# A conv, Fourier-mixing and FP8 network on one core: a shorter preparation and another order for the same pieces of work

## The chip, the cores and the metric

The kernel runs on one core of one Trainium2 chip. A core has five engines, each with its own in-order instruction stream: TensorE (PE) multiplies matrices into PSUM, VectorE (DVE) and ScalarE (ACT) do elementwise work, GpSimd (POOL) does elementwise work in SBUF alone, and SyncE (SP) issues transfers. ScalarE issues transfers too, from the same stream as its computing. PSUM has eight banks. The metric is device microseconds of one execution of the whole program; lower is better. The median of three runs of the kernel before is 4435.69 us (4433.55 to 4437.77).

## The reference, cut to what matters

For each of 32 images of 56 x 56 pixels and 96 channels there are two layers. The first is an inverted residual block whose weights are mixed per image from four experts; the second mixes the pixels by a Fourier transform and ends with a small feed-forward block in FP8.

```python
rw = sigmoid(mean(x, (1, 2)) @ Wr + br)                      # 4 weights per image
h = relu(bn(x @ mix(rw, Wpw)))                               # 96 -> 384 channels
h = relu(bn(sum_i rw[i] * (depthwise3x3(h, Wdw[i]) + bdw[i])))
x = bn(h @ mix(rw, Wpwl)) + x                                # 384 -> 96
t = to_tokens(x)
h = relu(bn(layernorm(t) @ w1.T))                            # 96 -> 192
X = fft(h, axis=tokens)                                      # 3136 tokens
y = ifft(relu(X.re*rd - X.im*id + rb) + 1j*relu(X.im*rd + X.re*id + ib)).real
t = t + bn(y @ w2.T)
t = t + q(relu(q(layernorm(t) @ q(W1).T) + b1) @ q(W2).T + b2)   # q: FP8 / FP16 rounding
```

## The kernel before, in words

**Preparation** (lines 350 to 618). The weights are loaded, the batch norms folded into them, and the results kept in SBUF for the whole run. Three parts of it matter here. The table `stk16` holds the depthwise taps, spread so that each of the 128 partitions has the taps of the pixel and channels that TensorE will need there. Its source is gathered straight from the input by 16 small loads into `raw` and 4 into `rawb`, and the batch-norm vectors are gathered in the same layout by 64 loads into `v2` (`v2f` in the profile) and 16 into `v2b` (lines 433 to 454); VectorE then scales (`s2f`, `s2b`) and spreads them into `wide` and `stk16` (lines 559 to 575). The second part packs the table of the first transform: two halves are loaded into `big`, packed into `small_a` and stored to the DRAM table `dad` (lines 484 to 494). The third is the expand weights `wpw_s`, whose bias rows and the vectors `bm` are loaded element by element (lines 461 to 473). All loads are issued by SyncE. The temporary tiles live in a pool that is released before the working tiles are allocated in the same memory, so each engine's first working instruction waits for the whole preparation.

**The work of an image** (`record`, from line 686). It is cut into 566 pieces, each a few instructions of one engine: ACT's copy of the input with its sum (`pad`), the mix of the weights (`mixed`, `mix_wk2`), the expand matmuls, the depthwise convolution by TensorE in four of six channel groups (`by_tensor`: GpSimd builds `wg`, ACT's transfers `hp<-h` and `h<-hp` regroup the data, `conv` multiplies) and by VectorE in two (`by_vector`: 32 `h<-h,small,h` instructions an image, the taps), the projection (`project`), the normalization (`moments`: `turn`, `stats`, `rest`, and `root` on GpSimd), the two transforms and the spectral step (`along_h`, `along_q`, `a1` to `a4` on ACT, `d1` to `d5` on VectorE, `second`, `back_q`, `back_h`), and the feed-forward (`up`, ACT's copy, VectorE's bias, GpSimd's cast `h<-h` to FP8, `down`, and GpSimd's addition `xs<-xs,y`). The images overlap.

**The order of the pieces.** `Plan.add` records a piece with its engine, a duration in microseconds written by hand, a wanted time (`due`), and what it reads, writes and takes from the rings of buffers. `Plan.order` then plays the plan: an engine that is free starts the ready piece with the earliest wanted time whose buffers are free. `LAG` is the delay from one engine to another. `HURRY` pulls readers of PSUM forward, so that banks come free. A piece that has waited longer than `PATIENCE` for a buffer keeps later ones from taking it. The wanted times start from `WANT`, with a period of 120 us an image. What the plan yields is only the order in which the instructions are emitted; on the chip, semaphores decide when each runs. Since each is emitted through one helper, nearly all have line 310 in the profile.

Of the kernel before, what the change touches and what calls it, by code (L numbers as in the profile page):

```python
# [11 lines left out]
F32 = mybir.dt.float32  # L12
# [6 lines left out]
NE = 4  # L19
C = 96  # L20
# [128 lines left out]
class Op:  # L149
    __slots__ = ("eng", "dur", "due", "emit", "bufs", "takes", "left", "ready", "after", "end", "seq", "size", "slack")  # L150
# [3 lines left out]
LAG = {"PE": 0.12, "DVE": 0.08, "ACT": 0.1, "POOL": 0.1, "SP": 0.15}  # L154
# [13 lines left out]
WANT = dict(period=120.0, expand=0.0, vector=1.4, forward=10.7, forward_step=27.0, freq=172.2,  # L168
            freq_step=7.0, tail=259.2, tail_step=26.5, x=17.0, mix=33.5, project=33.0)

HURRY = 40.0

PATIENCE = 4.8


class Plan:
    def __init__(self):
        self.ops = []
        self.writer = {}
        self.readers = {}  # L180
# [6 lines left out]
    def add(self, eng, dur, due, emit, reads=(), writes=(), takes=(), size=0):  # L187
        op = Op()
        if eng in ("DVE", "ACT") and any(isinstance(k[0], Buf) and isinstance(k[0].ring, Banks) for k in reads):
            due -= HURRY  # L190
        op.eng, op.dur, op.due, op.emit = eng, dur, due, emit
        op.takes, op.size, op.slack = list(takes), size, 0.0
        op.after, op.ready, op.end = [], 0.0, None
        op.seq = len(self.ops)
# [23 lines left out]
    def order(self):  # L218
# [4 lines left out]
        moved = 0.0  # L223
# [11 lines left out]
        def start(op, now):  # L235
            for b in op.takes:
                b.got = b.ring.take(b.n)
            op.end = now + op.dur
            free[op.eng] = op.end
            done.append(op)  # L240
            if op.size:
                nonlocal moved
                moved = max(moved, op.end + DMA_LAG) + op.size
                push(moved, "end", op)
            else:
                push(op.end, "end", op)
# [69 lines left out]
def kernel(  # L316
# [56 lines left out]
    nc.sync.dma_start(wr_s, wr)  # L373
    wpw_s = const([C + 1, NE + 1, M], F32, "wpw_s")
    nc.sync.dma_start(wpw_s[0:C, 0:NE], wpw)
# [38 lines left out]

    dad = dram.tile([PB, NQ, 2 * KR], F32, tag="dad", name="dad")

    with tc.tile_pool(name="prep", bufs=1) as pp:
        def temp(shape, name, dt=F32):
            return pp.tile(shape, dt, tag=name, name=name)


# [10 lines left out]
        raw = temp([128, 4, 9 * NT * NE], "raw")  # L432
        v2 = temp([128, 4, 4, NT], "v2f")
        rawb = temp([128, 4, NT * NE], "rawb")
        v2b = temp([128, 4, 4, NT], "v2b")
        lo = VECS["g2"][0]
        for r in range(4):
            for s in range(4):
                at = slice(32 * r + 8 * s, 32 * r + 8 * s + 8)
                nc.sync.dma_start(  # L440
                    raw[at], stk[:, 0 : 9 * NT, :].rearrange("(g c r) k e -> r c g (k e)", g=4, r=4)[r]
                )
                for k in range(4):
                    nc.sync.dma_start(
                        v2[at, :, k],
                        vecs[:, lo + NC3 * k : lo + NC3 * k + NT].rearrange("(g c r) k -> r c g k", g=4, r=4)[r],
                    )
        for q in range(4):
            nc.sync.dma_start(rawb[q::4], stk[:, 30 : 30 + NT, :].rearrange("(g r) k e -> g r (k e)", r=4))
            for k in range(4):  # L450
                nc.sync.dma_start(
                    v2b[q::4, :, k],
                    vecs[:, lo + NC3 * k : lo + NC3 * k + NT].rearrange("(g r) k -> g r k", r=4),
                )
        rawd = temp([128, 10, NE], "rawd")
        nc.sync.dma_start(rawd[:, 0:9], stk[:, 9 * DC : 9 * DC + 9, :])
        nc.sync.dma_start(rawd[:, 9:10], stk[:, 30 + DC : 31 + DC, :])
        row_s = temp([128, NROWS], "row_s")
        nc.sync.dma_start(row_s, rows.partition_broadcast(128))
        bm = temp([C + 1, 2, M], "bm")  # L460
        for j, name in enumerate(("b1", "m1")):
            lo, hi = VECS[name]
            nc.sync.dma_start(
# [4 lines left out]
        for e in range(NE):  # L468
            nc.sync.dma_start(
# [4 lines left out]
        bp = temp([128, NE], "bp")  # L474
        nc.sync.dma_start(bp, stk[:, NSTK - 1, :])
        nc.sync.dma_start(wpwl_s, wpwl)
        nc.sync.dma_start(w1c, w1t)
        for p in range(2):
            for ri in range(2):
                nc.sync.dma_start(  # L480
                    dftb_s[2 * p + ri :: 4], dftb[S * p + NQ * ri : S * p + NQ * ri + NQ]
                )
# [4 lines left out]
        for i in range(2):  # L487
            nc.sync.dma_start(big, dfta[:, i * (NQ // 2) : (i + 1) * (NQ // 2)])
# [5 lines left out]
            nc.sync.dma_start(dad[:, i * (NQ // 2) : (i + 1) * (NQ // 2)], small_a)  # L494
        nc.vector.memset(w2b, 0.0)
        nc.sync.dma_start(w2a[0:C], w2t[:, 0, :])
        nc.sync.dma_start(w2a[C:128], w2t[0:32, 1, :])
        for j in range(2):
            nc.sync.dma_start(w2b[64 * j : 64 * j + 64, j], w2t[32:C, 1, :])
        lo = VECS["rd"][0]  # L500
        nc.sync.dma_start(fa[0:C, 0:4], vecs[0:C, lo : lo + 8 : 2], allow_slow_non_contiguous=True)
        nc.sync.dma_start(fa[C:128, 0:4], vecs[0:32, lo + 1 : lo + 8 : 2], allow_slow_non_contiguous=True)
        for j in range(2):
            nc.sync.dma_start(
                fb[64 * j : 64 * j + 64, 0:4], vecs[32:C, lo + 1 : lo + 8 : 2], allow_slow_non_contiguous=True
            )
        nc.sync.dma_start(dftc_s, dftc)
        f1 = temp([C, M], "f1")
        nc.sync.dma_start(f1, fw1t)
        f2 = temp([128, NC3, C], "f2")  # L510
        nc.sync.dma_start(f2, fw2t)
# [20 lines left out]
        s2f = temp([128, 4, NT], "s2f")  # L532
        bn_scale(s2f, v2[:, :, 0], v2[:, :, 3], EPS_CONV)
        s2b = temp([128, 4, NT], "s2b")
        bn_scale(s2b, v2b[:, :, 0], v2b[:, :, 3], EPS_CONV)
        s2d = temp([128, 1], "s2d")
        bn_scale(s2d, vec("g2")[:, DC : DC + 1], vec("v2")[:, DC : DC + 1], EPS_CONV)
# [19 lines left out]

        nc.gpsimd.memset(stk16, 0.0)
        wide = temp([128, 4, NT, 4, 4, NE], "wide")
        nc.gpsimd.memset(wide, 0.0)  # L560
        for s in range(4):
            pw, ph = divmod(s, 2)
            for i in range(3):
                v = wide[:, :, :, 1 - pw + i, 1 - ph : 4 - ph, :].rearrange("p g c j e -> p (g c) (j e)")
                t = raw.rearrange("p g (c i j) -> p (g c) i j", i=3, j=3 * NE)[:, :, i, :]
                nc.vector.scalar_tensor_tensor(v, t, of_pixel[:, s : s + 1], v, ALU.mult, ALU.add)
        tap16 = stk16[:, :, 0 : 16 * NG].rearrange("p e (c g t) -> p e g c t", g=4, t=16)
        for t in range(16):
            bw, bh, qw, qh = t >> 3, t >> 2 & 1, t >> 1 & 1, t & 1
            for e in range(NE):  # L570
                nc.any.tensor_mul(tap16[:, e, :, :, t], wide[:, :, :, 2 * bw + qw, 2 * bh + qh, e], s2f)
        bias = stk16[:, :, 16 * NG : 17 * NG].rearrange("p e (c r) -> p e r c", r=4)
        for e in range(NE):
            nc.vector.tensor_mul(bias[:, e], rawb.rearrange("p r (c e) -> p r c e", e=NE)[:, :, :, e], s2b)
        bn_shift(bias[:, NE], v2b[:, :, 1], v2b[:, :, 2], s2b, "sh2")
        nc.vector.tensor_scalar_mul(stk16[:, 0:NE, 17 * NG], bp, s3)
        bn_shift(stk16[:, NE, 17 * NG : 17 * NG + 1], vec("b3"), vec("m3"), s3, "sh3")

        for e in range(NE):
            nc.vector.tensor_scalar_mul(stk16[:, e, NSM : NSM + 10], rawd[:, :, e], s2d)  # L580
        bn_shift(
            stk16[:, NE, NSM + 9 : NSM + 10], vec("b2")[:, DC : DC + 1], vec("m2")[:, DC : DC + 1], s2d, "sh2d"
# [27 lines left out]

        nc.vector.tensor_copy(fw1, f1, saturate=False)
# [74 lines left out]
    def record(b):  # L686
# [42 lines left out]
        def spread():  # L729
# [7 lines left out]
            "PE", 0.12, t0 - WANT["mix"] - 2,  # L737
# [17 lines left out]
        def mix_wk2():  # L755
# [8 lines left out]
            "DVE", 2.6, t0 - WANT["mix"], lambda: mixed(wk.ap, wpw_s, wpw_s[:, NE], C + 1),  # L764
# [3 lines left out]
            "DVE", 1.5, t0 - WANT["mix"], lambda: mixed(small.ap, stk16, stk16[:, NE], 128),  # L768
# [3 lines left out]
        add("DVE", 3.0, t0 + 5, mix_wk2, reads=[(mix, 2)], writes=[(wkc, 0)], takes=[wkc])  # L772
# [15 lines left out]
        def by_vector(h, c, due, acc):  # L788
# [42 lines left out]
            for i in range(2):  # L831
                parts = [(hv, k) for k in ((0, 1), (1, 2, 3))[i]]
                if i == 0:
# [3 lines left out]
                    "ACT", cols("ACT", T), at - 3, lambda i=i: first(i), reads=[*parts, (small, 0)],  # L837
                    writes=[(acc, i)], takes=[acc] if i == 0 else [],
                )
                for k, tap in enumerate((0, 1, 2, 3, 5, 6, 7, 8)):  # L840
                    add(
                        "DVE", 1.06, at + 2 * k, lambda i=i, tap=tap: one(i, tap), reads=[*parts, (small, 0)],
# [4 lines left out]
        def by_tensor(h, c, due, hid):  # L847
# [47 lines left out]
            def conv():  # L895
# [13 lines left out]
                "PE", 4.0, due, conv, reads=[(wg, 0), *((hp, r) for r in range(4))],  # L909
# [23 lines left out]
        for h in range(2):  # L933
# [36 lines left out]
            for c in range(NC3):  # L970
                add(
                    "PE", 3.0, due - (200 if c else 0), lambda c=c, f=project: f(c),
# [19 lines left out]
        def moments(p, of, key, due, out_extra):  # L992
# [27 lines left out]
            add("PE", 0.75, due, turn, reads=[key], writes=[(ps, 0)], takes=[ps, ln])  # L1020
            add("DVE", 1.26, due + 1, stats, reads=[(ps, 0)], writes=[(ln, 0)])
            add("DVE", 0.7, due + 1, rest, writes=[(ln, 0)])
            add("POOL", 2.1, due + 1, root, writes=[(ln, 0)])
# [3 lines left out]
        for st in range(NS):  # L1027
# [6 lines left out]
                "POOL", 1.2, due + 10,  # L1034
# [18 lines left out]
            for q0, nq in ((0, 4), (4, 3)):  # L1053
# [11 lines left out]
                def scaled(q0=q0, nq=nq, ps=ps, ha=ha, ln=ln):  # L1065
# [8 lines left out]
                    "PE", 0.31 * nq, due, hidden, reads=[(xh[h], k), (ln, 0)], writes=[(ps, 0)], takes=[ps, ha],  # L1074
                )
                add(
                    "DVE", 0.33 * nq, due + 1, scaled, reads=[(ps, 0), (ln, 0)], writes=[(ha, 0)],
# [3 lines left out]
                def along_h(q0=q0, nq=nq, ps=ps, ha=ha, da=da):  # L1081
# [11 lines left out]
                    "PE", 0.88, due + 3, along_h, reads=[(ha, 0), (da, 0), (da, 1)], writes=[(ps, 0)], takes=[ps, g],  # L1093
# [24 lines left out]
        for i, (k0, nk) in enumerate(GROUPS):  # L1118
# [12 lines left out]
            for blk, f, rz, n in ((0, fa, r_za, nk), (1, fb, r_zb, nb)):  # L1131
# [62 lines left out]
                ca, cd = cols("ACT", n * S), cols("DVE", n * S)  # L1194
# [5 lines left out]
                add("DVE", cd, due + 2 + blk, d1, reads=[(z, 0)], writes=[(tmp, 0)])  # L1200
                add("ACT", ca, due + 2 + blk, a4, writes=[(tmp, 1)])
                add("DVE", cd, due + 2 + blk, d4, reads=[(tmp, 0)], writes=[(z, 0)])
                add("DVE", cd, due + 3 + blk, d5, reads=[(tmp, 1)], writes=[(z, 1)])
# [299 lines left out]
```

## Time and profile before

| | |
|---|---|
| median of three runs | 4435.69 us |
| the profiled execution | 4425.4 us |
| its span, first to last instruction | 4423.4 us |
| TensorE busy | 4026.5 us (91%) |
| VectorE busy | 3599.7 us (81%) |
| ScalarE busy | 2517.5 us (57%) |
| GpSimd busy | 1763.6 us (40%) |
| mean granted TensorE clock | 0.954 |

A busy share is a mean over the whole span. The page also shows it in 40 slices of some 111 us as tenths, where 9 is 90% or more; the row PEclk shows the granted TensorE clock in the same slices. A row of waits names the waiting engine and what it writes, after the arrow the engine whose work ended the wait, and then the sum in microseconds, how often, and the longest. A row of a group gives the engine, the operation, its output and inputs, the shape, how often it ran, then busy time and the mean of one in ns, then the idle time before it. Names ending in "q" (SPq, ACTq) stand for the issuing of transfers.

### The profile page before, as it was taken

Reading aid. Unit: us, or ns where it says so; the run is one execution under the profiler, and the core shown is the slowest. Engines: PE = TensorE matmul, PEld = TensorE weight load, DVE = VectorE, ACT = ScalarE, POOL = GpSimd, SP = SyncE. Lnnn points to the kernel's source line nnn. Section 1 sums busy time; section 2 is a strip of 40 time slices with the busy share of each in tenths; the row PEclk is TensorE's granted clock in tenths of the full one; section 3 lists DMA queues with packets and bytes.
Section 4 is the critical chain, followed back from the end, with each engine's and each line's share of the span. In section 5 each row is a group of like instructions: output and inputs, shape, how many; then the busy total and the mean of one; then the engine's idle time right before and its main releaser. Section 6 shows DMA issues by size and latency. Waiting matters only on the chain.

```text
span 4423.4 us, 114239 instructions
## 1 busy us (share of the span) xinstructions
PE 4026.5 (91%) x44802; PEld 2551.4 (58%) x44802; DVE 3599.7 (81%) x9731; ACT 2517.5 (57%) x4971; POOL 1763.6 (40%) x1360
## 2 busy tenths in 40 slices
PE   1898999999999999999999999999999999999985
PEld 0465555665555665655565666566565566565563
DVE  5677788887788888888888888888888888878865
ACT  1365555566555666555656655565665555655553
POOL 1123444343444343444434444444444443444423
PEclk9898999999999999999999999999999999999997
DMA  3775877776877767787776787777678777677652
GB/s 79 135 168 142 182 175 165 166 163 159 180 176 160 172 168 166 181 178 164 172 170 158 177 183 182 162 173 163 163 176 180 165 163 163 162 170 173 157 140 73
DMA packets 441668, 719.40 MB, mean 163 GB/s; under 512 B 166090, under 2 KB 299530, under 8 KB 441130
## 3 DMA queue, kind: packets, MB, share of 16 engines
q1 hardware_dynamic: 391978, 495.24, 43.3%
q10 hardware_dynamic: 49152, 216.86, 27.1%
q8 instruction: 353, 5.78, 0.6%
q14 instruction: 185, 1.52, 0.1%
HBM read 286.08 MB, written 209.01 MB: 112 GB/s over the span
## 4 chain that ended last, share of the span: by engine, by line
PE 54%; DVE 14%; DMA 10%; ACT 9%; POOL 6%; issue 3%; SPq 2%; ACTq 1%; POOLq 0%; DVEq 0%
PE ps L310 54%; DVE h L310 4%; POOL h L310 3%; DVE ln L310 3%; DMA hp<-h 3%; DVE nt L310 3%; DMA out_dram<-xs 3%; POOL ln L310 2%; ACT tmpa L310 2%; DMA dd<-in_dftd_dram 2%; ACT h L310 1%; DMA xs<-xd 1%; ACT za L310 1%; ACTq L310 1%; ACT tmpb L310 1%
## 5 line engine op out<-in xcount | busy, mean ns | idle before, releaser
L310 DVE SCALAR_TENSOR_TENSOR h<-h,small,h 128x784 f32<-128x784 f32 x1024 | 1106.9, 1114 | 32.3 <-ACT h L310 24.4
L310 POOL CAST h<-h 128x784 fp8e5<-128x784 f16 x384 | 534.2, 1395 | 800.6 <-DVE h L310 790.2
L310 PE MATMUL ps<-x,wk 97*32 97x435 f32 (+2 forms) x4608 | 735.6, 601 | 17.0 <-DVE tmpb L310 13.1
L310 PE MATMUL ps<-hp,wg 32*32 32x392 f32 x16384 | 522.0, 515 | 38.6 <-issue 33.7
L310 POOL TENSOR_TENSOR xs<-xs,y 96x784 f32<-96x784 f32 x128 | 422.4, 3300 | 299.0 <-DVE y L310 277.1
L310 ACT ACTIVATE h<-ps 128x435 f32<-128x435 f32 (+2 forms) x768 | 400.4, 531 | 242.6 <-PE ps L310 225.0
L310 ACT ACTIVATE hp<-ps,small 128x392 f32<-128x392 f32 x512 | 267.2, 587 | 363.1 <-PE ps L310 274.8
L310 PE MATMUL ps<-dftb_s,g 112*64 112x112 f32 (+1 forms) x3776 | 416.3, 280 | 29.2 <-ACT tmpb L310 25.1
L310 POOL TENSOR_TENSOR ln<-ln,mhalf 120x7 f32<-120x7 f32 (+1 forms) x256 | 427.6, 1670 | 21.3
L310 DVE SCALAR_TENSOR_TENSOR ha<-ps,ln,nshift 120x192 f32<-120x192 f32 x896 | 306.4, 407 | 157.6 <-PE ps L310 153.1
L310 PEld LDWEIGHTS ps<-dftb_s,g 112*64 112x64 f32 (+1 forms) x3776 | 346.3, 167 | 142.4 <-issue 66.5
L310 POOL TENSOR_SCALAR ln<-ln 120x7 f32<-120x7 f32 (+1 forms) x256 | 89.3, 349 | 813.6 <-DVE ln L310 805.0
L310 PEld LDWEIGHTS ps<-hp,wg 32*32 32x32 f32 x16384 | 294.9, 105 | 202.0 <-issue 95.2
L310 PE MATMUL ps<-h,wk 32*96 32x392 f32 x4096 | 382.8, 519 | 0.7 <-DMA h<-hp 0.6
L310 DVE BATCH_NORM_STATS2 ln<-ps 120x6 f32<-120x96 f32 (+1 forms) x1792 | 318.0, 247 | 63.4 <-PE ps L310 63.2
L310 PEld LDWEIGHTS <-fw 96*128 96x128 fp8e5 (+1 forms) x1536 | 148.1, 113 | 369.7 <-issue 307.5
L310 ACT ACTIVATE h<-h 128x784 f32<-128x784 f32 x128 | 109.8, 858 | 439.4 <-DVE h L310 409.6
L310 PEld LDWEIGHTS ps<-x,wk 97*32 97x32 f32 (+1 forms) x4608 | 196.0, 122 | 277.5 <-issue 178.2
L310 ACT CAST h<-ps 128x784 f16<-128x784 f32 x384 | 305.3, 815 | 85.7 <-POOL h L310 65.5
L310 PE MATMUL ps<-w1c,x 96*120 96x192 f32 x1792 | 348.9, 342 | 2.7 <-DVE tmpb L310 1.0
L310 PEld LDWEIGHTS ps<-w1c,x 96*120 96x120 f32 x1792 | 302.4, 190 | 63.3 <-issue 30.7
L310 DVE TENSOR_SCALAR nt<-ps,ln 112x96 fp8e5<-112x96 f32 x896 | 266.8, 368 | 53.5 <-POOL ln L310 53.5
(178 smaller groups left out, 7275.4 us busy)
## 6 DMA issues: line engine op xcount, KB each, us to landing
hp<-h ACTq DMA_DIRECT2D x512, 217.5 KB
h<-hp ACTq DMA_DIRECT2D x512, 196.0 KB
gd<-g SPq DMA_DIRECT2D x384, 192.0 KB
g<-gd SPq DMA_DIRECT2D x192, 336.0 KB
dd<-in_dftd_dram SPq DMA_DIRECT2D x128, 343.0 KB
xd<-park SPq DMA_DIRECT2D x128, 294.0 KB
xs<-xd SPq DMA_DIRECT2D x128, 294.0 KB
yt<-yd SPq DMA_DIRECT2D x128, 294.0 KB
```

Of the source, the lines that this page charges most:

```text
L310: return self.tc.keep_in_program_order(method(*args, **kwargs))
```

## The change

The preparation takes the taps in one load, `rawp`, in the layout of the input; VectorE scales them there with the batch norm into `plain`, with the shift as a fifth column; `plain` goes to DRAM, and the 20 gathering loads read it back. The scaling after the spreading becomes a copy. The packing of `big` is written last, and most loads are issued by ScalarE.

In the plan, `port` marks VectorE's pieces with two SBUF inputs and all of GpSimd's, and only one of them runs at a time in the plan. Durations, lags, `HURRY`, `PATIENCE` and the period change, and a table `NUDGE` of 566 numbers is added to the wanted times, the same for each image. Which instructions an image consists of does not change.

```diff
-LAG = {"PE": 0.12, "DVE": 0.08, "ACT": 0.1, "POOL": 0.1, "SP": 0.15}
+LAG = {"PE": 0.1, "DVE": 0.06, "ACT": 0.06, "POOL": 0.08, "SP": 0.12}
-WANT = dict(period=120.0, ...
+WANT = dict(period=120.1, ...
-HURRY = 40.0
-PATIENCE = 4.8
+HURRY = 66.6
+PATIENCE = 1.6
+NUDGE = [
+    38, -0.7, 37.2, -3.6, -60, 38.9, -9, -64.3, 52.5, -3, 2.8, 5.8, 25, 15.7, -3.8, 2.9, -15.8, -29.5,
...
+]
     def add(self, eng, dur, due, emit, reads=(), writes=(), takes=(), size=0, port=False):
         op = Op()
+        op.seq = len(self.ops)
+        due += NUDGE[op.seq % len(NUDGE)]
...
+        op.port = port or eng == "POOL"
...
-            op.end = now + op.dur
+            if op.port:
+                nonlocal port
+                op.end = port = max(port, now) + op.dur
+            else:
+                op.end = now + op.dur
```

```diff
-        for r in range(4):
-            for s in range(4):
-                at = slice(32 * r + 8 * s, 32 * r + 8 * s + 8)
-                nc.sync.dma_start(
-                    raw[at], stk[:, 0 : 9 * NT, :].rearrange("(g c r) k e -> r c g (k e)", g=4, r=4)[r]
-                )
-                for k in range(4):
-                    nc.sync.dma_start(
-                        v2[at, :, k],
-                        vecs[:, lo + NC3 * k : lo + NC3 * k + NT].rearrange("(g c r) k -> r c g k", g=4, r=4)[r],
-                    )
...
+        rawp = temp([128, NSTK, NE], "rawp")
+        nc.sync.dma_start(rawp, stk)
         bm = temp([C + 1, 2, M], "bm")
...
-            nc.sync.dma_start(
+            nc.scalar.dma_start(
                 bm[C : C + 1, j].rearrange("o (c p) -> o c p", p=128),
...
-        nc.sync.dma_start(wpwl_s, wpwl)
-        nc.sync.dma_start(w1c, w1t)
+        nc.scalar.dma_start(wpwl_s, wpwl)
+        nc.scalar.dma_start(w1c, w1t)
...
-        for i in range(2):
-            nc.sync.dma_start(big, dfta[:, i * (NQ // 2) : (i + 1) * (NQ // 2)])
+        def pack(i):
+            nc.scalar.dma_start(big, dfta[:, i * (NQ // 2) : (i + 1) * (NQ // 2)])
...
+        for c in range(NT):
+            nc.vector.tensor_scalar_mul(plain[:, 9 * c : 9 * c + 9, 0:NE], rawp[:, 9 * c : 9 * c + 9], s2[:, c : c + 1])
+            nc.vector.tensor_scalar_mul(plain[:, 9 * NT + c, 0:NE], rawp[:, 10 * NC3 + c], s2[:, c : c + 1])
+        nc.vector.tensor_copy(plain[:, 9 * NT :, NE], sh2[:, 0:NT])
...
+        nc.sync.dma_start(plain_d, plain)
+        raw = temp([128, 4, 9 * NT, NE + 1], "raw")
+        rawb = temp([128, 4, NT, NE + 1], "rawb")
+        for r in range(4):
+            for s in range(4):
+                nc.sync.dma_start(
+                    raw[32 * r + 8 * s : 32 * r + 8 * s + 8].rearrange("c g k e -> c g (k e)"),
+                    plain_d[:, 0 : 9 * NT].rearrange("(g c r) k e -> r c g (k e)", g=4, r=4)[r],
+                )
+        for q in range(4):
+            nc.sync.dma_start(
+                rawb[q::4].rearrange("g r k e -> g r (k e)"),
+                plain_d[:, 9 * NT :].rearrange("(g r) k e -> g r (k e)", r=4),
+            )
...
+        for i in range(2):
+            pack(i)
```

```diff
-            "DVE", 2.6, t0 - WANT["mix"], lambda: mixed(wk.ap, wpw_s, wpw_s[:, NE], C + 1),
+            "DVE", 2.57, t0 - WANT["mix"], lambda: mixed(wk.ap, wpw_s, wpw_s[:, NE], C + 1), port=True,
-        add("DVE", 3.0, t0 + 5, mix_wk2, ...
+        add("DVE", 2.0, t0 + 5, mix_wk2, port=True, ...
-                        "DVE", 1.06, at + 2 * k, lambda i=i, tap=tap: one(i, tap), ...
+                        "DVE", 1.02, at + 2 * k, lambda i=i, tap=tap: one(i, tap), port=True, ...
-                "PE", 4.0, due, conv, ...
+                "PE", 3.75, due, conv, ...
-            add("POOL", 2.1, due + 1, root, writes=[(ln, 0)])
+            add("POOL", 1.8, due + 1, root, writes=[(ln, 0)])
-                "POOL", 1.2, due + 10,
+                "POOL", 0.84, due + 10,
-                ca, cd = cols("ACT", n * S), cols("DVE", n * S)
+                ca, cd = cols("ACT", n * S) + 0.06, cols("DVE", n * S) - 0.06
...
-                    "POOL", 1.1, due + 9.5,
+                    "POOL", 0.84, due + 9.5,
-                "POOL", 2.0, due + 15,
+                "POOL", 1.67, due + 15,
```

In the last part the three GpSimd durations are those of the copy to `park`, of the cast to FP8 and of the addition to `xs`; `d1`, `d4` and `d5` get `port=True`. The other durations on TensorE, of `turn`, `hidden`, `along_h`, `second`, `back_q`, `back_h`, `turn_back`, `up`, `down` and `project`, fall or rise by up to 20% in the same way.

## The prediction

> **What bounds the kernel now.** I read the page first, then a table by stretch of the span, then the waits of TensorE in the steady part, then the chain through the preparation, last GpSimd's operations by shape.
>
> The page, busy time and slices:
>
> ```profile
> span 4423.4 us, 114239 instructions
> PE 4026.5 (91%) x44802; PEld 2551.4 (58%) x44802; DVE 3599.7 (81%) x9731; ACT 2517.5 (57%) x4971; POOL 1763.6 (40%) x1360
> PE   1898999999999999999999999999999999999985
> PEclk9898999999999999999999999999999999999997
> ```
>
> TensorE is the bound everywhere but in the first slice (preparation) and the last two (drain). The table by stretch (columns: stretch, its length, busy PE, PEld, DVE, ACT, POOL, then granted clock, DMA share, GB/s):
>
> ```profile
> 0.00:60.00 60.00, 0.00 (x0) 0.00 (x0) 25.78 (x136) 3.21 (x10) 9.38 (x18) 1.00 0.25 51
> 60.00:100.00 40.00, 2.29 (x5) 1.40 (x6) 22.48 (x103) 4.97 (x10) 0.00 (x0) 1.00 0.46 122
> 1000.00:2000.00 1000.00, 946.42 (x10583) 596.31 (x10582) 842.50 (x2255) 601.24 (x1190) 418.45 (x318) 0.96 0.75 171
> 2000.00:3000.00 1000.00, 951.46 (x10674) 598.38 (x10673) 856.15 (x2261) 598.89 (x1171) 433.52 (x324) 0.97 0.74 171
> 3000.00:4000.00 1000.00, 939.36 (x10545) 599.82 (x10547) 838.32 (x2262) 600.42 (x1195) 413.81 (x314) 0.96 0.73 167
> ```
>
> So there are two things to win. One is the preparation: almost no TensorE work before 99 us. The other is 54.3 us of TensorE idle in each 1000 (mean of the three rows), and with it the clock. The granted clock is 0.963 there; if all busy time scaled with it, the missing 0.037 of 945.7 us is 35 us per 1000. The period of an image comes from the chain: its piece "13.40 PE ps x178" stands at 529.93 and again at 4079.37, 27 images later, so 131.5 us. Without idle and at full clock it would be 131.5 x (1 - 0.054 - 0.035) = 119.8 us. That is the floor, 11.7 us an image below now. What ends TensorE's idle time from 1000 to 4000 us:
>
> ```profile
> PE ps L310 <- POOL h L310: 41.7, 40, 1.7
> PE ps L310 <- DVE ln L310: 26.1, 24, 1.9
> PE ps L310 <- issue: 25.8, 17, 3.3
> PE ps L310 <- ACT tmpb L310: 17.7, 23, 1.4
> PE ps L310 <- ACT tmpa L310: 15.6, 22, 0.7
> ```
>
> None is long, and the counts (23 images lie in it) say that the same places stall in image after image: errors of a fixed order, not one missing resource. The largest is the last cast on GpSimd before the `down` matmuls. That cast and the residual addition, in the steady part (first two) and in the drain, where VectorE is mostly idle (last two):
>
> ```profile
> L310 POOL CAST h<-h 128x784 fp8e5<-128x784 f16 x276 | 399.6, 1452 | 580.7 <-DVE h L310 576.3 <-DMA da<-dad 4.3
> L310 POOL TENSOR_TENSOR xs<-xs,y 96x784 f32<-96x784 f32 x91 | 311.1, 3419 | 201.3 <-DVE y L310 191.9 <-DMA yt<-yd 9.4
> L310 POOL CAST h<-h 128x784 fp8e5<-128x784 f16 x18 | 15.9, 888 | 27.3 <-DVE h L310 27.3
> L310 POOL TENSOR_TENSOR xs<-xs,y 96x784 f32<-96x784 f32 x6 | 10.0, 1664 | 13.1 <-DVE y L310 13.1
> ```
>
> Beside VectorE they take 1452 and 3419 ns, alone 888 and 1664. The plan of before counts 1.1 and 2.0 us, so it is short by 0.35 and 1.4 us where it matters.
>
> The chain of the preparation:
>
> ```profile
> 66.47 5.07 DMA big<-in_dfta_dram
> 76.96 5.91 DMA big<-in_dfta_dram
> 87.93 2.86 DMA dad<-small_a
> 99.23 1.11 PE ps L310
> ```
>
> Until 66.5 us the chain is SyncE issuing small transfers one after another; then two loads of `big`, two packings on VectorE (4.9 us each), two stores; at 91.05 the first instruction of the plan may start, and it waits for all of the preparation.
>
> **What the Trainium skill says.** GPSIMD Engine Reference, "8. Key points": it shares its SBUF interfaces with VectorE and contends with instructions of two SBUF inputs. The four rows above agree (1452 against 888 ns). TensorE: Matmul & The Clock Gate, "HAM oscillation — how this bites in real kernels": idle gaps let the array's clock fall. The trace agrees in sign: 0.963 in the steady part, 0.67 from 4350 to 4400 us, where gaps of 2 to 4 us lie. DMA: Bandwidth & Descriptors, "Two DMAs through the same engine are not ordered": a transfer that reads another's output has to wait for its completion; `raw<-plain_d` will do so.
>
> **The change, part by part.** First the preparation. Removed are 80 small loads of `v2f` and `v2b`, 20 of `raw` and `rawb` from the input, `rawd` and `bp`: SyncE's 3.98 to 49.2 us and 60.3 to 62.2 us. Added are one load `rawp`, a scaling on VectorE into `plain`, its store, 20 loads from it. 25 loads move to ACT's queue. I walk the new order with durations of the rows of before.
> - ACT's queue: `bm` and the bias rows of `wpw_s` 10.6 us (49.71 to 60.32 before), `wpwl_s` to `dftb_s` 4.2, `w2a` to `f` 6.8, some 2.5 of waits for earlier transfers: done at 24. Then one table load (1.28) and the square roots (1.9): 27.4; `big` is issued behind them at 28 and lands at 33.
> - VectorE in its order waits for `fa`, `fb`, `f1`, `f2`, so it reaches the reciprocals at 26.9. Reciprocals and products 8 us, five 0.56 us products for `wpw_s`, some ten operations of 0.15 to 0.2: `plain` is ready at 39.4.
> - Store and landing 1.8 (as `wd<-wkc`: 104.11 to 105.93): 41.2. Loads of `raw` at 0.33 each. Meanwhile VectorE scales `wpwl_s` and the rest (5.3) and packs the first half of `big` (4.9): 49.6.
> - The second load of `big` waits for that packing and takes 5.4: 55. Here is a wait that the diff doesn't show: each transfer waits for the one eight places before it in issue order, and the fifteenth load of `raw` follows `big` on the same semaphore. So two loads of `raw` and all four of `rawb` (0.6 each) sit behind it on SyncE until 58.2, and the first store of `dad`, in the same queue, until 61.4.
> - `wide` then runs 57.8 to 61 and the copies to 61.7. The second packing needs the first store landed and ends at 66.6; the second store takes 3.2: 69.8.
> The plan would start at 70 instead of 91: 21 us less. Bounds: without that coupling 64 (27 less); with slower loads on ACT's queue and one more landing of 2 to 3 us at each of three dependent steps 78 (13 less). Nothing covers or hides this stretch, so it goes to the end in full.
>
> Second, the plan. No instruction of the 32 images changes in kind or size: 566 pieces an image in both. What changes is their order, through four inputs. Exclusion with the durations of a free port: VectorE's port pieces are 32 x 1.02 + 2.57 + 2.0 + 12.7 (three of the nine pieces of a spectral step, by `cols` less 0.06) = 50 us an image, GpSimd's 8 x 1.8 + 12 x 0.84 + 4 x 1.67 + 4 x 0.84 + 4.4 + 0.5 = 39. Together 89 of a period of 120, so the rule fits. GpSimd was busy 422 us in 1000, 55 us an image: 16 us of stretching that the old plan knew only as flat averages. TensorE's pieces get durations near the rows (`conv` 3.75; its 128 records span 3.6 to 3.7 at full clock). The lags fall by 0.02 to 0.04 us, `HURRY` rises and `PATIENCE` falls, and a table moves each piece's wanted time by 16 us on average. I can't read a time out of an order. Bounds from the trace: nothing (the new order stalls as often), and all of 11.7 us an image. I take half. The stalls recur in the same places, which is what an order with truer durations removes; but of the idle listed above only the GpSimd row and part of the ACT and VectorE rows stand where the plan's numbers were wrong, DMA is busy 0.74 of the time with its model unchanged, and VectorE at 84% leaves little room to catch up. Half is 5.9 us x 31 periods = 183 us. Fill and drain (99 to 240 us and 4211 to the end) I leave, at 10 us either way: chains of single pieces there.
>
> Sum, against the profiled execution: span 4423.4 - 21 - 183 = 4219. Its own time was 4425.4, and the median of the runs shown is 10.3 above that; carried over, 4435.7 - 204 = 4232.
>
> **Rivals.**
> - *Preparation alone.* The order is different and not better. For: the places that wait by ACT and VectorE are short chains that any dense order meets again. Against: the GpSimd waits. 4435.7 - 21 = 4415, from 4395 to 4423.
> - *Nearly the floor.* The search found an order that the chip follows; 0.85 of 363 us: 4435.7 - 21 - 309 = 4106. For: recurrent stalls, and a clock that rises as gaps close. Against: DMA and VectorE as above.
> - *Slower.* VectorE falls behind a plan that counts its taps at 1.02 us, where the row shows 1114 ns: 32 x 0.094 = 3 us an image. If these do not overlap idle time, the projections, which wait for the taps, stand 3 us each image: 31 x 3 - 21 = 72 us more, 4508. It decides from 0.7 us an image on (21 / 31). Against: exclusion already books GpSimd's time on the same port, and VectorE has 16% idle to give.
> - *The preparation does not shrink*, as `plain_d` adds a dependent trip: only with the upper bounds twice over; not separate.
>
> **How the numbers follow.** Half, meaning a gain of 2.5 to 8.5 us an image: 0.60, 4152 to 4340. Nearly the floor 0.16. Preparation alone or little more (to 2.5 us) 0.16. Slower 0.08. The range 4115 to 4400 leaves out about 0.08 below and 0.12 above. A run tells 0.2%, 9 us, from no change: faster 0.90, same 0.02, slower 0.08.
>
> **What would show it.** First plan instruction near 70 us, with `raw`'s last loads behind the second `big`; the period 125 to 126 us; TensorE idle near 27 us in 1000 with a clock of 0.98; the wait for POOL `h` gone from the head of the list; POOL's cast nearer 1.1 us. Wrong: a period of 131, or of 121; new waits of TensorE by DMA.

## The result and the profile after

| | before | after |
|---|---|---|
| median of the runs, us | 4434.62 | 4577.98 |
| profiled execution, its own time / its span, us | 4425.4 / 4423.4 | 4554.42 / 4552.7 |
| first instruction of the plan, us | 91.05 | 72.98 |
| period of an image, us | 131.5 | 137.45 |
| TensorE idle in 1000 us of the steady part | 54.3 | 76.8 |

The changed kernel is slower: ratio 1.0324, 95% interval 1.0275 to 1.0373. The forecast was 4232 us.

The period is read in every kernel from the one `pooled` piece on VectorE that each image has: in after it starts at 1020.2 and, 22 images later, at 4044.2 us. 31 periods that are 6.0 us longer make 185 us more, and the preparation 18 less. Fill and drain are shorter: span less start less 31 periods is 219 us in after and 256 in before. Together 185 - 18 - 37 = 130, as the two spans have it (129.3); the medians differ by 143.

The page of after, its busy times and slices:

```profile
span 4552.7 us, 114486 instructions
PE 4085.5 (90%) x44802; PEld 2665.0 (59%) x44802; DVE 3500.7 (77%) x9663; ACT 2521.9 (55%) x4982; POOL 1710.1 (38%) x1361
PE   2999999999998999999999999999999999999985
PEclk9999999999998999999999999998999999999986
```

TensorE got its first work earlier (a 2 in the first slice), and its busy time rose by 59 us with the same 44802 matmuls. The table by stretch (stretch, length, busy PE, PEld, DVE, ACT, POOL, granted clock, DMA share, GB/s) says that the clock fell too:

```profile
0.00:60.00 60.00, 0.95 (x2) 0.40 (x2) 30.30 (x115) 2.68 (x8) 9.60 (x19) 1.00 0.39 96
1000.00:2000.00 1000.00, 918.39 (x10064) 598.90 (x10067) 776.08 (x2126) 567.29 (x1123) 387.41 (x302) 0.93 0.69 160
2000.00:3000.00 1000.00, 924.96 (x10220) 607.49 (x10198) 791.80 (x2211) 580.15 (x1150) 395.40 (x309) 0.94 0.70 162
3000.00:4000.00 1000.00, 926.40 (x10320) 605.73 (x10310) 787.83 (x2152) 565.80 (x1112) 402.04 (x308) 0.94 0.71 164
```

All engines do less in 1000 us, and TensorE is still the busiest of them. What ends TensorE's idle time from 1000 to 4000 us (total, times, longest):

```profile
PE ps L356 <- DVE tmpa L356: 66.0, 43, 2.5
PE ps L356 <- ACT g L356: 57.2, 21, 4.5
PE ps L356 <- DVE ha L356: 40.8, 65, 1.1
PE ps L356 <- ACT h L356: 21.7, 24, 1.2
```

The wait for GpSimd's `h`, 41.7 us before, is gone, and its cast is short; both were forecast (the cast and the residual addition by shape: count, then busy us and mean ns):

```profile
L356 POOL TENSOR_TENSOR xs<-xs,y 96x784 f32<-96x784 f32 x88 | 387.2, 4400 | 256.3 <-DVE y L356 256.3
L356 POOL CAST h<-h 128x784 fp8e5<-128x784 f16 x261 | 273.4, 1051 | 921.3 <-DVE h L356 901.9 <-DVE mix L356 19.4
```

In their place stand other waits, again about as many as there are images or a small multiple: a new order with stalls of its own at fixed places. The addition takes 4400 ns, longer than the 3419 of before, where the plan, with the exclusion of the port, counts 1670.

The preparation did what was forecast. SyncE's issues in after:

```profile
44.49 0.35 SPq L592 DMA_DIRECT2D plain_d<-plain  x1
46.06 12.95 SPq L597 DMA_DIRECT2D raw<-plain_d  x16
59.05 2.56 SPq L602 DMA_DIRECT2D rawb<-plain_d  x4
61.71 8.53 SPq L514 DMA_DIRECT2D dad<-small_a  x2
72.98 1.60 SPq L356 DMA_DIRECT2D da<-dad  x4
```

The sixteen loads of `raw` take 12.95 us, held behind the second `big` as the walk had it, and the plan's first instruction comes at 72.98, 3 us after the forecast.

One more view differs more than any other. ScalarE's waits that a transfer ended, from 1000 to 4000 us; in before the largest are

```profile
ACT hp L310 <- DMA h<-hp: 38.2, 6, 7.1
ACT h L310 <- DMA hp<-h: 16.2, 4, 5.5
```

and 82 us in all; in after

```profile
ACT h L356 <- DMA yt<-yd: 79.5, 11, 7.5
ACT h L356 <- DMA g<-gd: 72.5, 18, 4.7
ACT g L356 <- DMA h<-hp: 49.8, 10, 5.9
ACT h L356 <- DMA hp<-h: 44.8, 11, 8.5
```

and 295 us in all. One such place, in ScalarE's order of time (start, duration, what, idle time before):

```profile
2191.96 7.72 ACTq L356 DMA_DIRECT2D hp<-h  x5
2199.73 1.61 ACT L356 ACTIVATE h<-h 128x784 f32<-128x784 f32 x2 [7.24 <-DMA yt<-yd]
```

`hp<-h` doesn't read `yt`. In the compiled program the transfers of SyncE and ScalarE take eight semaphores in turn, and one that gets a semaphore waits for its last user, eight places earlier in the common order of issue. The trace shows it here: the last of the five `hp<-h` has the semaphore of a `yt<-yd` that landed at 2199.16, and is issued at 2199.18. The Trainium skill, DMA: Bandwidth & Descriptors, "Why a DMA increments its semaphore by 16 and not by 1", gives a reason for such a wait: with two transfers in flight on one semaphore, a count doesn't tell which has landed. The traces show the wait; no run here leaves it out. ScalarE stands still meanwhile, and its evictions stand behind it.

### The profile page after: what moved, and what is told of

The parts are those of the page before. It is cut to its first block, busy times and chain, and to the rows that moved or that the text cites. A ratio compares the mean times of both kernels' runs of the same rounds, so it can differ in the third digit from the quotient of the medians.

```text
span 4552.7 us, 114486 instructions
## 1 busy us (share of the span) xinstructions
PE 4085.5 (90%) x44802; PEld 2665.0 (59%) x44802; DVE 3500.7 (77%) x9663; ACT 2521.9 (55%) x4982; POOL 1710.1 (38%) x1361
## 4 chain that ended last, share of the span: by engine, by line
PE 63%; DVE 13%; DMA 8%; ACT 6%; issue 4%; POOL 3%; ACTq 2%; SPq 1%; POOLq 0%; DVEq 0%
PE ps L356 63%; DMA yt<-yd 5%; DVE ha L356 3%; DVE nt L356 3%; POOL xs L356 2%; DVE h L356 2%; ACT h L356 2%; ACTq L356 1%; ACT tmpa L356 1%; DVE za L356 1%; DMA out_dram<-xs 1%; DVE tmpa L356 1%; DMA hp<-h 1%; ACT tmpb L356 1%; DVE zb L356 1%
## 5 line engine op out<-in xcount | busy, mean ns | idle before, releaser
L356 POOL CAST h<-h 128x784 fp8e5<-128x784 f16 x384 | 395.7, 1034 | 1304.2 <-DVE h L356 1278.5
L356 PE MATMUL ps<-x,wk 97*32 97x435 f32 (+2 forms) x4608 | 686.4, 570 | 3.2 <-DVE wk L356 3.2
L356 POOL TENSOR_TENSOR xs<-xs,y 96x784 f32<-96x784 f32 x128 | 531.2, 4150 | 376.7 <-DVE y L356 373.5
L356 PE MATMUL ps<-hp,wg 32*32 32x392 f32 x16384 | 562.2, 558 | 23.6 <-issue 13.2
L356 PEld LDWEIGHTS ps<-hp,wg 32*32 32x32 f32 x16384 | 324.0, 109 | 204.4 <-issue 124.4
L356 PE MATMUL ps<-dftb_s,g 112*64 112x112 f32 (+1 forms) x3776 | 440.0, 291 | 1.5 <-ACT hp L356 1.1
L356 PEld LDWEIGHTS ps<-dftb_s,g 112*64 112x64 f32 (+1 forms) x3776 | 369.5, 176 | 109.0 <-issue 47.9
L356 POOL TENSOR_TENSOR ln<-ln,mhalf 120x7 f32<-120x7 f32 (+1 forms) x256 | 396.3, 1548 | 21.3
L356 ACT ACTIVATE tmpa<-ps,fa 128x224 f32<-128x224 f32 (+1 forms) x448 | 210.7, 499 | 206.7 <-PE ps L356 199.2
L356 PE MATMUL ps<-dd,yt 116*96 116x112 f32 x1792 | 241.3, 297 | 80.2 <-ACT g L356 71.7
```

What stands on the lines that cost most here:

```text
L356: return self.tc.keep_in_program_order(method(*args, **kwargs))
```

## The experiments

The planner is arithmetic over its durations, so each kernel also has a planned period: from where the plan ends images 3 and 28. "Gap" is the measured period less the planned one. Half clock is the time from 1000 to 4000 us in which the trace's clock record grants TensorE 0.5. `e_plan`, `e_actsp_tap` and the two runs with an added stall are given below. A run's profiled execution need not be its median, so small differences of period and of median do not match exactly.

| kernel | median us | planned period | period | gap | TensorE idle in 1000 | half clock, us |
|---|---|---|---|---|---|---|
| before | 4434.6 | 127.9 | 131.5 | 3.6 | 54.3 | 215 |
| after | 4578.0 | 128.6 | 137.45 | 8.8 | 76.8 | 396 |
| e_prep | 4409.3 | 127.9 | 131.2 | 3.3 | 53.7 | 208 |
| e_prep_actsp | 4337.1 | 127.9 | 129.8 | 2.0 | 49.6 | 212 |
| e_actsp | 4461.7 | 128.6 | 134.0 | 5.4 | 61.4 | 379 |
| e_dur | 4583.0 | 128.4 | 137.05 | 8.6 | 76.2 | 263 |
| e_durport | 4689.4 | 135.8 | 140.7 | 4.9 | 86.2 | 393 |
| e_nonudge | 4687.0 | 134.7 | 140.8 | 6.1 | 88.4 | 372 |
| e_jit_a | 4429.9 | 130.0 | 133.1 | 3.1 | 58.9 | 184 |
| e_jit_b | 4629.3 | 133.3 | 139.7 | 6.4 | 89.8 | 369 |
| e_pe | 4646.6 | 133.6 | 139.5 | 6.0 | 86.4 | 348 |
| e_peold | 4517.4 | 131.9 | 135.0 | 3.0 | 75.5 | 215 |

**The two parts apart.** `e_prep` is before with the hunks of the diff inside and just ahead of the `prep` pool; `e_plan` is before with all the others.

> The new preparation with the plan of before, instruction for instruction. My step for the preparation, corrected by the trace of after (first instruction of the plan at 73 instead of 91 us): 4434.6 - 18 = 4417 us, period of an image unchanged at 131.5 us. If the new preparation had a cost later on (where its constants lie, what its transfers leave behind for the first images), the time would be 4430 or more.

> The new plan with the preparation of before. If the two parts add up, 4578 + 18 = 4596 us, with the period of 137.5 us that the trace of after shows. If the plan was harmed by what the new preparation left behind, it would come out at 4450 or less.

Measured: `e_prep` 4409.3 us, ratio to before 0.9942 (0.9922 to 0.9962); `e_plan` 4584.6 us, 1.0349 (1.0315 to 1.0383), period 137.8. The preparation gains 17 to 35 us and does no harm later; the whole loss is the plan's. The question is what in the plan loses 4578.0 - 4409.3 = 169 us against `e_prep`.

**ScalarE behind its own transfers.** The order of all engines stays; only the issuing queue changes:

```diff
-                    lambda r=r: se.dma_start(
+                    lambda r=r: sy.dma_start(
                         hp.ap[32 * r : 32 * r + 32].rearrange("p g n -> p (g n)"), hg.ap[r::4, :]
...
-                    lambda q=q: se.dma_start(
+                    lambda q=q: sy.dma_start(
                         hid.ap[32 * q : 32 * q + 32].rearrange("p r n -> p (r n)"),
```

> The changed kernel with the same order on every engine, but the transfers between h and hp that ScalarE issues are issued by SyncE, at their place in the plan's order. Theory A (ScalarE stands in its queue behind its own transfers, each waiting for an earlier one: 295 us of such waits from 1000 to 4000 in after, 82 in before, and its evictions then come late to TensorE): the period falls from 137.5 to about 131, 4578 - 6 x 31 = about 4390 us, unless SyncE now holds other transfers back. Theory B (the waits of ScalarE are cover, the order itself stalls TensorE): 4530 to 4620 us, with TensorE's waits for tmpa, g and ha as in after.

> The control of e_actsp: the plan of before and the new preparation (e_prep, 4409 us), with the transfers between h and hp issued by SyncE. Theory A (ScalarE standing behind its own transfers is what the new order made worse): the old order has few such waits (98 us from 1000 to 4000 in e_prep, 295 in after), so the gain is small, 10 to 40 us: 4370 to 4400. Theory S (any order gains by taking these transfers off ScalarE, and e_actsp says nothing on the change): about the 116 us that after gained, near 4295 us.

Measured: `e_actsp` 4461.7 us, 116 less than after; `e_prep_actsp` 4337.1 us, 72 less than `e_prep` and 0.9774 (0.9740 to 0.9808) of before: the fastest kernel of this study. Both lie between their two theories. ScalarE's waits for transfers fall to 65 and 8 us. What ended TensorE's idle time in `e_actsp`:

```profile
PE ps L356 <- DVE tmpa L356: 69.8, 46, 2.5
PE ps L356 <- DVE ha L356: 51.0, 67, 1.1
PE ps L356 <- issue: 27.2, 17, 3.6
PE ps L356 <- ACT h L356: 23.0, 25, 1.0
PE ps L356 <- DVE nt L356: 14.6, 44, 0.5
```

The wait for `g`, 57 us, is gone; those for `tmpa`, `ha` and `nt` are as in after. Without the control, theory A would seem nearly right. With it, most of the gain turns out to be open to the old order too: of the 169 us only 116 - 72 = 44 come from the new order meeting these waits more often. The other 4461.7 - 4337.1 = 125 us are in the order itself. The edit takes two things off ScalarE at once, the waits and the issuing (392 us of its queue from 1000 to 4000 in after, 428 in `e_prep`); no run parts them.

In the plan one can see what `tmpa` is. TensorE's `up` wants two neighbouring PSUM banks; a forward transform has just taken one of them, and `up` stands until VectorE has evicted it. The stall is in the plan's own arithmetic, 2.44 us once in each image, and on the chip; TensorE's order of time in `e_actsp`:

```profile
997.45 0.92 PE L356 MATMUL ps<-dftb_s,g 112*128 112x112 f32 x6
1000.88 1.46 PE L356 MATMUL ps<-n,fw 96*128 96x392 fp8e5 x4 [2.51 <-DVE tmpa L356]
```

It is not a surprise to the plan, but an order that it made.

**The steps of the plan, one after the other.** `e_dur` is `e_prep` with the new durations, lags and period only; `e_durport` adds the exclusion; `e_nonudge` adds the new `HURRY` and `PATIENCE`; the table makes it after.

> The new preparation with only the new durations and lags in the plan: no exclusion, no table, HURRY and PATIENCE as before. This is the step of my prediction on its own: an order made with truer durations. Theory M (mine: truer durations remove recurring stalls): a period below 131.2 us and a time below the 4409 us of e_prep, about 4320 if it is half of what I took. Theory P (what the plan's own clock does not know, transfers and clock, stays, and shorter TensorE pieces take away its reserve): planned period 128.4 plus a gap of 3.6 to 6 us, so 132 to 134.4 us, 4430 to 4510 us.

> e_dur with the exclusion of the shared port added to the plan, still without the table and with HURRY and PATIENCE as before. The plan's own clock gives a period of 135.8 us instead of 128.4. Theory X (the exclusion books time that the chip does not lose, and the order follows the plan): 135.8 + 3.6 to 6 us a period, 4650 to 4730 us. Theory Y (the exclusion is true, and what it books the chip loses anyway): the gap to the plan closes, 136 to 137 us, at the level of e_dur if e_dur has 136 too, else 4560 us.

> The changed kernel without its table: NUDGE is not added to the wanted times; exclusion, durations, lags, HURRY and PATIENCE stay. The plan's own clock gives 4423 us for it, against 4219 with the table and 4229 for before; the chip needed 3.6 us an image more than the plan for before and 8.9 more for after. Theory T (the table fits the plan's arithmetic and not the chip): without it the chip follows the plan as closely as it did before, 134.7 + 3.6 = 138.3 us an image, about 4600 us. Theory D (the gap of 8.9 us comes with the exclusion and the durations): 134.7 + 8.9 = 143.6 us an image, about 4760 us.

```diff
 e_durport against after
-        due += NUDGE[op.seq % len(NUDGE)]
-HURRY = 66.6
-PATIENCE = 1.6
+HURRY = 40.0
+PATIENCE = 4.8
 e_dur against e_durport
-        op.port = port or eng == "POOL"
+        op.port = False
```

Measured, step by step: durations and lags +174 us (4583.0), exclusion +106 (4689.4), `HURRY` and `PATIENCE` -2 (4687.0, no difference), table -109 (4578.0). So the durations, which my forecast counted on, cost more than the whole loss, and more than either theory had: M was below 4409, P ended at 4510. The exclusion comes on top, and theory X holds for it: it books time. It doesn't keep the pieces apart on the chip either: GpSimd's addition takes 2535 ns with it and 2458 without. `e_nonudge` falls between theories T (4600) and D (4760). The table is no mere misfit: it wins 109 us, though the plan's own clock promised 204. Each step makes a new order, so these figures belong to this sequence of steps; the next runs show how much an order alone can do.

**Why truer durations lose.** Two runs change nothing but the wanted times, by at most 0.3 us; two split the durations.

```diff
 e_jit_a, e_jit_b against e_prep (566 random numbers from -0.3 to 0.3 in JIT)
+        due += JIT[len(self.ops) % 566]
 e_pe against e_prep (twelve such edits)
-                "PE", 4.0, due, conv, reads=[(wg, 0), *((hp, r) for r in range(4))],
+                "PE", 3.75, due, conv, reads=[(wg, 0), *((hp, r) for r in range(4))],
 e_peold against e_dur: the same twelve, back
```

> e_prep (4409 us, 131.2 us an image) with each piece's wanted time moved by a random amount of at most 0.3 us, the same for all images; durations, lags, HURRY and PATIENCE of before. The plan's own clock gives 130.0 us an image instead of 127.9. Theory Q (the order of before is a picked one: the smallest change of the wanted times reorders everything and costs time, whatever the durations say): 130.0 plus a gap of 3.6 to 8.9 us, 133.6 to 138.9 us, 4485 to 4650 us. Theory N (0.3 us of wanted time are nothing to the chip; what e_dur lost came from its durations): 4385 to 4435 us.

> As e_jit_a with other random amounts, also at most 0.3 us; the plan's own clock gives 133.3 us an image. Theory Q: 136.9 to 142.2 us an image, 4585 to 4750 us. Theory N: 4385 to 4435 us.

> e_prep with only the new durations of TensorE's pieces in the plan (122.9 us of TensorE planned in an image before, 117.7 now); no other new duration, lag, exclusion or table. The plan's own clock gives 133.6 us an image. Theory P (the longer pieces are a reserve that keeps the chip near its plan; without it the gap widens to that of e_dur, 8.6 us): 142.2 us an image, about 4750 us. Theory Q (the gap has nothing to do with TensorE's durations): 3.6 to 6 us of gap, 137 to 139.5 us, 4590 to 4670 us.

> e_dur with the durations of TensorE's pieces as before: new are those of VectorE, ScalarE and GpSimd and the lags. The plan's own clock gives 131.9 us an image. Theory P: the gap goes back to 3.6 us, 135.5 us an image, about 4545 us, below e_dur's 4583 although its plan is longer by 3.5 us an image. Theory Q: a gap of 5 to 9 us like that of other orders, 137 to 141 us, 4590 to 4710 us.

Measured: `e_jit_a` 4429.9, `e_jit_b` 4629.3, `e_pe` 4646.6, `e_peold` 4517.4 us. `e_jit_a` came out where theory N had it and below theory Q. But `e_jit_b` is 220 us slower than `e_prep` though no wanted time moved by more than 0.3 us and no duration changed. Its waits of TensorE begin with one stall of 4.5 us in every image:

```profile
PE ps L314 <- DVE tmpa L314: 103.4, 23, 5.0
PE ps L314 <- DVE ln L314: 50.2, 45, 1.3
PE ps L314 <- ACT g L314: 48.5, 19, 4.2
```

So theory N falls. The planner is greedy, and each image's pattern is repeated 32 times: a minute change at one decision gives another pattern, here 20 and 220 us worse. Both random tables give planned periods above the 127.9 of before, 130.0 and 133.3 us. That fits an order of before that was picked among many, a pick that new durations lose; with two tables it is not shown. The durations don't add up either: those of TensorE alone cost 237 us (`e_pe`), the others alone 108 (`e_peold`), both together 174.

Theory P holds in part. `e_peold` came out where P had it. The gap is 2.0 to 3.6 us for five of the six kernels planned with the old durations of TensorE and 4.9 to 8.8 for the six planned with the new ones. But `e_jit_b`, with the old ones, has 6.4, and `e_pe`, for which P expected 8.6, has 6.0. Much of the gap is in TensorE's busy time; this is accounting, not an experiment. The pieces add up to 122.9 us an image with the old durations and to 117.7 with the new ones. On the chip (idle column and period) an image takes 0.923 x 137.45 = 126.9 us of TensorE in after, 124.4 in before. If TensorE is busy all through the half clock, it loses half of that time: 396 / 2 / 3000 x 137.45 = 9.1 us an image in after, an estimate, which leaves 117.8. So the new durations are true, at full clock; the chip runs 132 of 1000 us at half clock, and the plan doesn't know it. The old ones were too long by somewhat less than what the clock takes in before (3.2 against 4.7 us).

Idle time completes the account. In after the plan has TensorE idle for 128.6 - 117.7 = 10.9 us an image and the chip for 10.6, so there the whole gap is busy time. `e_durport` plans 18.1 us of idle and has 12.1: where a plan has more idle time, part of the longer busy time fits into it. And in `e_dur` the clock explains only 6.0 of 8.9 us of longer busy time; the rest stays open.

**VectorE.** One of the eight taps that VectorE does for a piece is not issued, in the order of `e_actsp`; the output lacks that term.

```diff
-                        "DVE", 1.02, at + 2 * k, lambda i=i, tap=tap: one(i, tap), port=True, reads=[*parts, (small, 0)],
+                        "DVE", 1.02, at + 2 * k, lambda i=i, tap=tap: one(i, tap) if tap != 3 else None, port=True, reads=[*parts, (small, 0)],
```

> e_actsp (4462 us, period 134.0 us) with one of the eight VectorE taps of each piece not issued, so that part of the depthwise sum is left out: 4 x 1.1 = 4.4 us of VectorE less in each image, in the same order. My rival Slower (VectorE falls behind a plan that counts its taps at 1.02 us): the rest of the loss goes, the period falls to about 131 us and the time to about 4370. Theory B (the order itself waits for PSUM banks and for short chains at fixed places, and the clock falls after these): 4430 to 4465 us, TensorE's waits for tmpa, ha and nt as in e_actsp.

Measured: 4454.1 us, period 133.7, against 4461.7 and 134.0. The taps that stay grow from 1120 to 1174 ns, so VectorE's busy time falls by 2.4 us an image (3494.2 to 3418.8 us), not by 4.4, and that brings 0.3: my rival's mechanism is not at work in this order. GpSimd's addition falls from 3486 to 1851 ns in the same run, so its length isn't what the order waits for either.

**One added stall.** The base is `e_prep_actsp`. Ahead of the first conv of an image ScalarE copies a small tile onto itself eight times, and TensorE runs one matmul of four columns, into the bank that conv then overwrites; in `e_hold` that matmul reads the copied tile, in `e_free` another.

```diff
+            for _ in range(8):
+                se.copy(pad, pad)
+            te.matmul(ps.bank()[:C, 0:NE], pad[0:96], pad[0:96, 0:NE], start=True, stop=True)
```

> e_prep_actsp (4337 us, 129.8 us an image) with eight small copies added on ScalarE ahead of the first conv of each image (about 2 us of ScalarE) and one tiny matmul on TensorE that waits for none of them. The control of e_hold: what the copies alone cost. ScalarE is idle 40% there, so 0 to 1 us an image: 4337 to 4370 us.

> e_free, but the tiny matmul reads what the eight copies write, so TensorE stands still once in each image, at the first conv, for some 2 us. Theory K (a stall costs more than its own length, because stretches of half clock follow it): against e_free, 2 us of stall and 2 to 5 us of clock an image, 31 x 4 to 7 = 124 to 217 us more, and more half-clock stretches between 1000 and 4000 us (27 in e_prep_actsp, 61 in after). Theory L (a stall costs at most its own length; TensorE catches up later): 0 to 2 us an image, 0 to 62 us more, and as many half-clock stretches.

Measured: 4344.9 us, as expected, and 4466.0, 121 us apart, or 3.9 us for each of 31 periods (3.1 by the periods of the two traces). The stall was longer than meant; the waits of TensorE in `e_hold`:

```profile
PE ps L310 <- ACT pad L310: 93.3, 22, 4.4
PE ps L310 <- POOL h L310: 46.2, 46, 1.8
PE ps L310 <- issue: 5.2, 5, 1.8
```

It is 4.24 us each time, and in exchange 22 us of waits put down to issue go (27.5 in `e_free`), so 3.2 us an image are net. The number lies just under theory K's 124 to 217 us, and that for a stall twice as long as K reckoned with: a stall costs about its own net length, nothing of it is caught up, and the clock adds little. Half-clock stretches do become more, 42 instead of 29, but half clock only goes from 222 to 263 us, and (263 - 222) / 2 / 3000 x 133 = 0.9 us an image. The Trainium skill (TensorE: Matmul & The Clock Gate, "HAM oscillation — how this bites in real kernels") warns of idle gaps above about 3.4 us; one of 4.2 us in 133 us shows the sign, not the doubling of after.

The traces say more on the doubling. In all sixteen of them the clock record changes only on a fixed grid of 3.41 us. I sort the grid's windows between 1000 and 4000 us that begin at full clock by whether TensorE is busy for less than 0.6 of the window:

| kernel | windows under 0.6 | of these, half clock follows | other windows | of these, half clock follows |
|---|---|---|---|---|
| before | 26 | 24 | 789 | 6 |
| after | 52 | 47 | 709 | 14 |
| e_free | 30 | 26 | 783 | 2 |
| e_hold | 47 | 39 | 754 | 3 |

So what goes with half clock is a thinly used window. A single gap of 3.4 us is not needed: before has none above 3.3 us there, and its clock still falls 30 times. After has twice as many such windows as before, and 1.8 times the half clock.

## Why the prediction was wrong

**Preparation: right.** 18 us of the 21, within its bounds; `e_prep` confirms it alone. ScalarE's queue took until 31 instead of 24 us and `plain_d` was issued at 44.5 instead of 39.4; the rest of the walk, with the coupling of `raw` to the second `big`, took up part of it.

**The step that failed** is "I take half": that the stalls recur in the same places, "which is what an order with truer durations removes", 5.9 us an image less. The period became 6.0 us longer. Four things were wrong in it.
- Recurring stalls are not a sign of wrong durations. Every order here, repeated image after image, has recurring stalls, whichever durations it was made with; the largest new one, for `tmpa`, is in the plan's own arithmetic. `e_dur` shows the step alone: +174 us.
- The plan could have been asked beforehand. Half of 11.7 us meant a period of 125.6 us, but by its own arithmetic the new plan has 128.6, against 127.9 for the old one, although TensorE's pieces are 5.2 us an image shorter in it. It has TensorE idle for 10.9 us an image instead of 5.0; on the chip it was 10.6 instead of 7.1. The idle time that I took away was planned in.
- The lower bound of the plan's effect was set at "nothing". An order can be worse, and `e_jit_b` shows by how much without any reason in its durations: 220 us. Only the rival "Slower" had a loss, for another reason; both signs belonged in the sum.
- "TensorE's pieces get durations near the rows ... at full clock" was read as a gain in truth. Against `e_prep`, an image of after has 3.5 us more of TensorE idle and an estimated 9.1 - 4.6 = 4.5 us more lost to half clock, with 1.8 us less of busy time beyond that: 6.2 together. The plan accounts for none of the clock.

**The wait that I had and didn't carry on.** The semaphore eight places back is in my walk of the preparation; in the steady part ScalarE waits 295 us in 3000 for transfers, and I named DMA only as "its model unchanged". My sign of a wrong forecast was a new wait of TensorE by DMA; the new waits by DMA are ScalarE's. Taking these transfers off ScalarE is worth 44 us of the change's loss, and 72 in the old order, where TensorE's list of waits didn't show them.

**Right and worthless:** the wait for GpSimd's `h` went, and its cast took 1051 ns.

**The rivals.** "Slower" came nearest in number (4508), by luck: `e_actsp_tap` does not find its mechanism. "Preparation alone" (4415) is what `e_prep` is.

**What stays open.** Which waits make the thinly used windows of after, and what fewer of them would bring; the table of windows is a reading of traces, and only `e_hold` tests it. And the 125 us of the order are split by accounting, not by an experiment: 134.0 - 129.8 is 1.8 us more of idle and 2.4 of busy time.

## What to carry to other kernels

An order made by a greedy planner can be a draw: before a change to its inputs is credited or blamed, move an input by next to nothing and see how far the time moves. Ask the planner for its own period first. A forecast for a re-planned kernel needs both signs.

An engine that issues transfers between its computations takes their waits into its own queue; here these were partly for transfers that it had nothing to do with. Moving the issue to a queue that computes nothing gave 72 and 116 us here with no other edit; look for it in the waits of the issuing engine, not of the bottleneck.

## What the hardware showed beyond expectation

TensorE's clock record knows two values in the steady part, 1 and 0.5, and the half-clock stretches last 3.4, 6.8 or 10.2 us, seldom longer multiples of 3.4 (to 20.5). Taken out at half their length, they leave 117.3 to 121.2 us of TensorE an image in all twelve kernels of the first table of the experiments, while busy time itself runs from 123.4 to 128.6 with the same matmuls. So a mean duration depends on the order around it, and the clock accounts for only part of that spread.
